# Denominators of two token tiles summed by ScalarE, eight staging places, and the copy of the denominators on VectorE, in a one-core attention and quantized-FFN layer

## The chip, the cores and the metric

The kernel runs on one core of a Trainium2 chip. A core has a matrix engine (TensorE, PE in the profile; its weight loads are listed as PEld), VectorE (DVE), ScalarE (ACT), GpSimd (POOL) and SyncE (SP, which here issues nearly all transfers). Each engine works through its own instructions in order and waits on semaphores of the others. The work memory SBUF and the matrix engine's result memory PSUM both have 128 partitions; PSUM has eight banks of 512 float32 columns.

The metric is the time of the whole kernel on the device in microseconds, the median of several executions. Lower is better.

## What is computed

The input x has 4 batches of 512 tokens with 1024 features. One attention block and one quantized linear layer, each behind a layer norm and with a residual:

```python
q = (ln(x) @ Wq).reshape(b, s, 32, 32)         # 32 heads of 32
k, v = split(ln(x) @ Wkv)                      # one key and one value head for all
scores = einsum('bqhd,bkd->bhqk', q, k) * 32 ** -0.5
scores = where(causal, scores + slope[h] * (pos_k - pos_q), -inf)
attn = softmax(scores, axis=-1)
x = x + einsum('bhqk,bkd->bqhd', attn, v).reshape(b, s, h) @ Wo
w = (unpacked_6bit_codes - zero_point) * scale # 1024 x 1024
x = x + (ln(x) @ w.T + bias)
```

All tensors are float32. The kernel gets that accuracy by splitting operands into a high and a low part and adding two or three products.

## The kernel before

A batch has 4 token tiles of 128 tokens (NT = 4). The 32 heads form 8 groups of 4 (GH = 4, NG = 8). A batch and a group make one *step*; there are 32 steps, and after them 16 token tiles of the output projection and the linear layer. Work of neighbouring steps, of the next batch's preparation and of the first token tiles overlaps.

One step does this:

- `queries` (line 749) computes the group's queries, and their high and low parts go through DRAM into a stacked tile `qs`, below which lie rows that add the position bias and the causal mask of whole key blocks.
- `maxima` (line 806) computes the scores with queries on the partitions: for each token tile t and head h a tile of 128 queries by (t + 1) x 128 keys, in a PSUM bank `s` (two banks). On each tile one VectorE instruction (line 837) adds the mask to the scores, writes the negated sum to `junk` and puts the negated row maximum into a column of `mx`. `mx` is transposed by PE (line 862), split into a high and a low part by ScalarE (line 868, tile mt0) and VectorE (line 873, tile mt1), and both rows are sent by DMA into `qs`, so that the next product has the maximum already subtracted.
- `attention` (line 891) computes the scores again, with the keys on the partitions: key block j against queries j x 128 to 511, into PSUM banks `st` (two banks, line 913). ScalarE takes the exponential into the tiles p0 to p3 (line 923), GpSimd zeroes the part above the diagonal (line 932), and PE multiplies with the values (line 942, `pav`), four heads side by side on four column tiles.
- The softmax denominators come from two places. For the last token tile (queries 384 to 511) ScalarE takes the exponential of the `junk` that line 837 left in a staging tile, with the maximum as bias and with a running sum as second output (line 852), into a column of `own_den`. For the other 384 queries GpSimd adds p1 and p2 onto p0 (line 955, two additions: 4 x 256 and 4 x 128 columns), PE sums over the partitions with a matrix of ones (line 970, `den`, 4 heads x 384 columns), ScalarE copies the result out of PSUM (line 977), and a DMA writes it to `den_d` in DRAM (line 980).
- `invert` (line 984) runs once per batch: PE transposes `own_den`, ScalarE copies it (line 996), a DMA writes these rows to `den_d` (line 999), all denominators of the batch are read into `rec` (line 1007), inverted by VectorE (line 1013) and written to `rden_d` (line 1017).
- `token_tile` (line 1118) multiplies the attention output by these reciprocals and does the output projection (line 1170), the layer norm and the linear layer (line 1289).

Tiles come from pools with a fixed number of buffers. The pool `stg` ("staging", 5 places of 128 x 512 float32) is shared: weights on their way in, `junk` of the last token tile, the attention output `a`, the denominators `d`, codes, and the linear layer's products. `mt` holds two buffers each of mt0 and mt1; `rec` and `zs` (the zero points) have places of their own.

The order of the instructions is not written by hand. Every operation is entered with a due time (in units where a step takes 15), an estimated cost and the tiles it reads and writes. `order` (line 368) lays all operations out by a model of the engines, with 16 different small shifts of the due times, and takes the best by its model. It fixes the order on every engine and on the DMA queue, and which earlier user of a buffer a new one waits for. So an edit of a cost or of a pool size changes the order of the whole program.

The instruction that makes the staged scores and the row maximum, shared by both kernels, in its essence:

```python
nc.vector.tensor_tensor_reduce(
    out=junk()[:, :W], in0=ps()[:, o : o + W], in1=mask()[:, S - W :],
    scale=-1.0, scalar=3e38, op0=ALU.add, op1=ALU.min,
    accum_out=mx()[:, h * NT + t : h * NT + t + 1],
)
```

Of the kernel before, what the change touches and what calls it, by code (L numbers as in the profile page):

```python
# [34 lines left out]
F32 = mybir.dt.float32  # L35
# [4 lines left out]
AF = mybir.ActivationFunctionType  # L40
# [4 lines left out]
P = 128  # L45
NH = 32
HD = 32
GH = 4
S = 512
H = 1024  # L50
# [346 lines left out]
def layer_kernel(  # L397
# [29 lines left out]

    for name, bufs in (
        ("const", 1), ("w", 2 * NG), ("xc", KC + 2), ("x", 4), ("qs", 3), ("q1", 1), ("p0", 2),
        ("pj", 1), ("stg", 5), ("kv", 2), ("small", 4), ("mt", 2), ("rec", 1), ("zs", 1),  # L430
    ):
        pool(name, bufs)
    for name, bufs in (("s", 2), ("st", 2), ("m", 4)):
# [2 lines left out]
    def new(pool_name, tag, shape, dt, name):  # L436

        p, bufs = pools[pool_name]
        return work.item(lambda: p.tile(shape, dt, tag=tag, name=name), (pool_name + tag, bufs))
# [13 lines left out]
    def act(at, n, fn, out, ins, sbuf=False):  # L453
        work.op("ACT", at, n / 1.2 + (90.0 if sbuf else 70.0), fn, out, ins)
# [212 lines left out]
    kv = {}  # L667
# [134 lines left out]
    ROWS = (0, 1, 2, "b")  # L802

    own_den = {}

    def maxima(at, i):
        b = i // NG
        k = kst[b % 2]
        mx = new("small", "mx", [P, GH * NT], F32, f"mx_{i}")
        if i % NG == 0:  # L810
            own_den[b] = new("small", "sump", [P, GH, NG], F32, f"dn_{b}")
        for n, bank in enumerate(S_BANKS):
            ps = new("ps_s", "s", [P, S], F32, f"s_{i}_{n}")
            widths = [(t + 1) * P for t, _ in bank]
            places = [sum(widths[:m]) for m in range(len(bank))]

            def products(ps=ps, bank=bank, widths=widths, places=places):
                for (t, h), W, o in zip(bank, widths, places):
                    q, at = part(i, h)
                    nc.tensor.matmul(  # L820
                        ps()[:, o : o + W], q()[0:R_MAX, at, ts(t, P)], k()[0:R_MAX, :W],
                        start=True, stop=True,
                    )
            pe(
                at + 1.2 * n, widths, products, [ps],
                [
                    (part(i, h)[0], (r, h) if i < DIRECT and r != "b" else r)
                    for _, h in bank for r in ROWS
                ] + [k],
                more=5.0,  # L830
            )
            for (t, h), W, o in zip(bank, widths, places):
                kind = ("stg", "stg") if t == NT - 1 else ("q1", "junk")
                junk = new(*kind, [P, S if t == NT - 1 else S - P], F32, f"junk_{i}_{t}_{h}")
                dve(
                    at + 1.2 * n + 0.3, W,
                    lambda ps=ps, junk=junk, t=t, h=h, W=W, o=o: nc.vector.tensor_tensor_reduce(  # L837
                        out=junk()[:, :W],
                        in0=ps()[:, o : o + W],
                        in1=mask()[:, S - W :],  # L840
                        scale=-1.0,
                        scalar=3e38,
                        op0=ALU.add,
                        op1=ALU.min,
                        accum_out=mx()[:, h * NT + t : h * NT + t + 1],
                    ),
                    [(mx, (t, h)), junk] if t == NT - 1 else [(mx, (t, h))], [ps], more=125.0,
                )
                if t == NT - 1:
                    act(  # L850
                        at + 1.2 * n + 2.0, S + 130,
                        lambda junk=junk, h=h, t=t: nc.scalar.activation(  # L852
                            junk(), junk(), AF.Exp, bias=mx()[:, h * NT + t : h * NT + t + 1],
                            scale=-1.0, accum_out=own_den[b]()[:, h, i % NG : i % NG + 1],
                        ),
                        [junk, (own_den[b], (h, i % NG))], [junk, (mx, (t, h))], sbuf=True,
                    )
        at += 1.2 * len(S_BANKS)
        N = GH * NT
        tr = new("ps_m", "m", [P, P], F32, f"trm_{i}")  # L860
        pe(
            at, [P], lambda: nc.tensor.transpose(tr()[0:N, :], mx(), ident()), [tr], [mx]
        )
        for s in range(2):
            m = new("mt", f"mt{s}", [N, P], F32R, f"mt{s}_{i}")
            if s == 0:
                hi = m
                act(at + 0.2, P, lambda: nc.scalar.copy(hi(), tr()[0:N, :]), [hi], [tr])
            else:
                lo = m  # L870
                dve(
                    at + 0.4, P,
                    lambda: nc.vector.tensor_tensor(
                        lo(), tr()[0:N, :], hi().bitcast(F32), ALU.subtract
                    ),
                    [lo], [tr, hi],
                )
            for h, n, q in qs[i]:
                dma(
                    at + 0.5 + 0.2 * s, 2e3 * n,  # L880
                    lambda m=m, s=s, h=h, n=n, q=q: move(
                        q()[R_MAX + s : R_MAX + s + 1, :, :], m()[h * NT : (h + n) * NT, :]
                    ),
                    [(q, f"m{s}")], [m],
                )
# [5 lines left out]
    def attention(at, i):  # L891
# [54 lines left out]
        for js, when in (((0, 1), 10.4), ((2, 3), 14.4)):  # L946
# [1 line left out]
                at + when, [4.0 * (S - j * P) for j in js], lambda js=js: products(js), [pav],  # L948
                [kv[b]] + [pr[j] for j in js], tiled=True,
            )  # L950
        L = S - P
        for j in range(1, NT - 1):
            def add(j=j):
                d = pr[0]()[:, :, j * P : L]
                nc.gpsimd.tensor_tensor(d, d, pr[j]()[:, :, 0 : L - j * P], ALU.add)  # L955
            pool_op(
                at + (0, 11.4, 15.0, 15.4)[j], 140.0 + 2.16 * GH * (L - j * P), add,
                [pr[0]], [pr[0], pr[j]],
            )
# [14 lines left out]
        pe(at + 20.0, [4.0 * L], sums, [d], [pr[0]], tiled=True)  # L974

        kept = new("stg", "stg", [P, L], F32, f"d_{i}")
        act(at + 25.5, L, lambda: nc.scalar.copy(kept(), d()), [kept], [d])
        dma(
            at + 26.0, 8e3,
            lambda: nc.sync.dma_start(out=den_d[b, :, g, 0:L], in_=kept()[0:P:HD, :]),  # L980
# [3 lines left out]
    def invert(at, b):  # L984

        tr = new("ps_m", "m", [P, P], F32, f"trd_{b}")
        N = GH * NG
        pe(
            at - 14.0, [P],
            lambda: nc.tensor.transpose(  # L990
                tr()[0:N, :], own_den[b]().rearrange("p h g -> p (h g)"), ident()
            ),
            [tr], [own_den[b]],
        )
        rows_ = new("mt", "mt0", [N, P], F32, f"rows_{b}")
        act(at - 13.5, P, lambda: nc.scalar.copy(rows_(), tr()[0:N, :]), [rows_], [tr])
        dma(
            at - 13.0, 16e3,
            lambda: nc.sync.dma_start(
                out=den_d[b].rearrange("h g q -> (h g) q")[:, S - P :], in_=rows_()  # L1000
            ),
            [(den_i[b], "own")], [rows_],
        )
        r = new("rec", "rec", [P, P], F32, f"rec_{b}")
        dma(
            at, 65e3,
            lambda: nc.sync.dma_start(
                out=r(), in_=den_d[b].rearrange("h g (c q) -> (h g c) q", q=P)
            ),
            [r], [den_i[b]],  # L1010
        )
        work.op(
            "DVE", at + 2.5, 840.0, lambda: nc.vector.reciprocal(r(), r()), [r], [r],
        )
        dma(
            at + 4.0, 65e3,
            lambda: nc.sync.dma_start(
                out=rden_d[b].rearrange("h g (c q) -> (h g c) q", q=P), in_=r()
            ),
            [rden_i[b]], [r],  # L1020
        )
# [60 lines left out]
    def ffn_rows(early, at, later):  # L1082

        b1 = new("pj", "p1", [P, 2, HALF], F32, "bias")
        b2 = [new("q1", t, [P, HALF], F32, f"scale_{t}") for t in ("qh", "ql")]
        b3 = new("zs", "zs", [P, 2, HALF], F32, "zs")
        scale = w_scale.rearrange("n o -> (n o)")
        for when, o, size, ap, src in (
            (early, b3, 524e3, lambda: b3().rearrange("p a b -> p (a b)"),
             w_zero.rearrange("n o -> (n o)")),  # L1090
            (at, b2[0], 262e3, b2[0], scale[0:HALF]),
            (at, b2[1], 262e3, b2[1], scale[HALF:H]),
            (later, b1, 524e3, lambda: b1().rearrange("p a b -> p (a b)"), ffn_bias),
        ):
            dma(
                when, size,
                lambda ap=ap, src=src: nc.sync.dma_start(
                    out=ap(), in_=src.partition_broadcast(P)
                ),
                [o], [],  # L1100
            )
        rows["bias"] = [(b1, lambda n=n: b1()[:, n, :]) for n in range(2)]
        rows["scale"] = [(b2[n], b2[n]) for n in range(2)]
        rows["zs"] = [((b3, n), lambda n=n: b3()[:, n, :]) for n in range(2)]
        for n in range(2):
            it, ap = rows["zs"][n]
            dve(
# [315 lines left out]
```

## Time and profile before

| What | Value |
|---|---|
| Median of 3 runs | 810.4 us (809.18, 811.1, 810.4) |
| The profiled execution | 812.18 us |
| Its span, first to last instruction | 810.5 us |
| Mean granted clock of TensorE | 0.997 |
| Line 837 (row maxima, DVE), 512 instructions | 247.5 us busy |
| Line 923 (exponentials, ACT), 352 | 184.5 us busy |
| Line 852 (exponentials with sum, ACT), 128 | 92.0 us busy |
| Line 955 (additions of p, POOL), 64 | 118.1 us busy |
| Line 970 (den, PE), 256 | 27.2 us busy |
| Line 977 (copy of den, ACT), 32 | 15.6 us busy |

The profile was taken from one execution, of 812.18 us; its times are not those of the runs of the median. The page gives the busy time of each engine, the span in 40 slices, the transfers, the chain of work that ended last (followed back from the last instruction, at each step to what released it) and the costliest groups of instructions by line, with their number, their busy time, the mean duration of one in nanoseconds, and the idle time of the engine before them. Two views cut the span into stretches: busy time of every engine in each. The durations of neighbouring rows overlap, on PE and on ScalarE above all, so that a row's duration is longer than the time that it takes from its engine; the distance from one start to the next is the latter.

By slices of 20 us, in tenths, the engines' busy shares are:

```profile
PE   5999989999999999999999999999999999999997
DVE  7576758566777466876476667546876657676765
ACT  5667966778888677898687786541232323332320
POOL 5137633534644333643537684665726535455333
```

Steps run to about 550 us, and the token tiles fill the rest.

### The profile page before, as it was taken

What the parts mean: (1) busy time and instruction counts of PE and PEld (TensorE: products, weight loads), DVE (VectorE), ACT (ScalarE), POOL (GpSimd) and SP (SyncE); (2) the same over time, 40 slices, a digit from 0 to 9 for tenths busy, and PEclk for the clock granted to TensorE, in tenths of its full rate; (3) what the DMA queues carried; (4) which work ended last, traced back from release to release, by engine and by line L of the source; (5) the groups of instructions that cost most, each with busy time, mean ns of one, the idle gap of its engine ahead of it and who ended that gap; (6) DMA issues with size and microseconds to landing.
All of it is one profiled execution on the core that took longest, in us unless ns stands there. A gap on an engine that the chain in (4) does not pass through costs nothing.

```text
span 810.5 us, 13698 instructions
## 1 busy us (share of the span) xinstructions
PE 790.3 (98%) x4468; PEld 591.5 (73%) x4468; DVE 538.3 (66%) x1484; ACT 477.0 (59%) x961; POOL 403.9 (50%) x397
## 2 busy tenths in 40 slices
PE   5999989999999999999999999999999999999997
PEld 4675667677666777677776767677888888888886
DVE  7576758566777466876476667546876657676765
ACT  5667966778888677898687786541232323332320
POOL 5137633534644333643537684665726535455333
PEclk9999999999999999999999999999999999999999
DMA  7257655765834764734767885748666755657321
GB/s 225 57 142 208 181 162 137 202 187 149 240 106 122 202 190 144 233 118 131 202 182 181 241 226 144 249 109 216 183 151 167 153 137 124 160 138 179 86 53 65
DMA packets 131815, 131.31 MB, mean 162 GB/s; under 512 B 42980, under 2 KB 94436, under 8 KB 130720
## 3 DMA queue, kind: packets, MB, share of 16 engines
q1 hardware_dynamic: 131392, 128.49, 58.0%
q0 software_dynamic: 352, 1.96, 0.9%
q8 instruction: 35, 0.57, 0.3%
q14 instruction: 36, 0.29, 0.1%
HBM read 84.27 MB, written 39.06 MB: 152 GB/s over the span
## 4 chain that ended last, share of the span: by engine, by line
PE 90%; DMA 3%; DVE 3%; ACT 1%; issue 1%; POOL 1%; SPq 0%; DVEq 0%; POOLq 0%
PE pq L757 21%; PE po L1170 19%; PE pf L1289 13%; PE st L913 10%; PE s L820 10%; PE pav L942 9%; PE den L970 3%; PE pkv L674 2%; PE tr L656 2%; DVE junk L837 1%; DMA rec<-den_d 1%; DMA wq_st<-in_L_attn_Wq_dram 1%; DMA raw<-rden_d 1%; DMA rden_d<-rec 1%; ACT qs L733 1%
## 5 line engine op out<-in xcount | busy, mean ns | idle before, releaser
L837 DVE CUSTOM_DVE_ANT_0 junk<-s,mask 128x512 f32<-128x512 f32 (+3 forms) x512 | 247.5, 489 | 126.0 <-PE s L820 100.1
L923 ACT ACTIVATE p<-st 128x512 f32<-128x512 f32 (+1 forms) x352 | 184.5, 559 | 65.0 <-PE st L913 60.7
L757 PE MATMUL pq<-xc,wqh 128*128 128x512 f32 x512 | 198.5, 404 | 0.0
L932 POOL TENSOR_SCALAR_AFFINE_SELECT p<-p 128x512 f32<-128x512 f32 x128 | 83.3, 653 | 201.8 <-ACT p L923 195.8
L1170 PE MATMUL po<-woh,aT 128*128 128x512 f32 x512 | 165.4, 391 | 0.0
L820 PE MATMUL s<-kst,qs 124*128 124x512 f32 (+3 forms) x512 | 130.2, 325 | 5.5 <-DMA wq_st<-in_L_attn_Wq_dram 1.6
L913 PE MATMUL st<-qs,kst 126*128 126x512 f32 (+1 forms) x352 | 128.8, 398 | 0.6 <-DMA qs<-mt 0.5
L955 POOL TENSOR_TENSOR p<-p,p 128x1024 f32<-128x1024 f32 x64 | 118.1, 1845 | 12.5 <-PE pav L942 11.7
L820 PEld LDWEIGHTS s<-kst,qs 124*128 124x128 f32 x512 | 91.6, 189 | 40.1 <-DVE mx L837 9.9
L1289 PE MATMUL pf<-wf,xT 128*128 128x512 f32 x512 | 120.5, 391 | 0.1
L757 PEld LDWEIGHTS pq<-xc,wqh 128*128 128x128 f32 x512 | 97.3, 190 | 21.5 <-issue 2.2
L1170 PEld LDWEIGHTS po<-woh,aT 128*128 128x128 f32 x512 | 96.2, 188 | 20.0 <-issue 0.6
L1289 PEld LDWEIGHTS pf<-wf,xT 128*128 128x128 f32 x512 | 95.8, 188 | 20.4 <-DVE xT L473 0.6
L757 PE MATMUL pq<-xc,wql 128*128 128x512 f32 x256 | 101.3, 396 | 0.0
L852 ACT ACTIVATE junk<-junk,mx 128x512 f32<-128x512 f32 x128 | 92.0, 721 | 13.9 <-DVE mx L837 11.3
L1170 PE MATMUL po<-wol,aT 128*128 128x512 f32 x256 | 99.8, 390 | 0.0
L913 PEld LDWEIGHTS st<-qs,kst 126*128 126x128 f32 x352 | 64.1, 189 | 25.9 <-ACT p L923 6.6
L942 PE MATMUL pav<-p,kv 128*32 128x512 f32 (+3 forms) x1024 | 80.8, 437 | 0.3 <-POOL p L932 0.3
L1309 POOL TENSOR_TENSOR x<-x,y 128x512 f32<-128x512 f32 x30 | 42.7, 1426 | 60.8 <-DVE y L1300 58.9
L942 PEld LDWEIGHTS pav<-p,kv 128*32 128x32 f32 x1024 | 28.1, 109 | 44.0 <-issue 30.8
L1170 PEld LDWEIGHTS po<-wol,aT 128*128 128x128 f32 x256 | 48.2, 188 | 9.4
L757 PEld LDWEIGHTS pq<-xc,wql 128*128 128x128 f32 x256 | 49.2, 192 | 6.4
(92 smaller groups left out, 903.2 us busy)
## 6 DMA issues: line engine op xcount, KB each, us to landing
qs<-q_d SPq DMA_DIRECT2D x90, 256.0 KB
x<-_attn_hidden_states_dram SPq DMA_DIRECT2D x31, 512.0 KB
at_d<-a SPq DMA_DIRECT2D x32, 256.0 KB
raw<-at_d SPq DMA_DIRECT2D x16, 512.0 KB
raw<-rden_d SPq DMA_DIRECT2D x64, 128.0 KB
out_dram<-x SPq DMA_DIRECT2D x32, 256.0 KB
q_d<-qh SPq DMA_DIRECT2D x30, 256.0 KB
q_d<-ql SPq DMA_DIRECT2D x30, 256.0 KB
```

The source lines that it names most:

```text
L757: nc.tensor.matmul(pq(), w()[:, c, :], xc[b, c]()[:, s, :], start=(c == 0 and n == 0), stop=(c == KC - 1 and n == 2),)
L820: nc.tensor.matmul(ps()[:, o : o + W], q()[0:R_MAX, at, ts(t, P)], k()[0:R_MAX, :W], start=True, stop=True,)
L837: lambda ps=ps, junk=junk, t=t, h=h, W=W, o=o: nc.vector.tensor_tensor_reduce(out=junk()[:, :W], in0=ps()[:, o : o + W], in1=mask()[:, S - ...
L852: lambda junk=junk, h=h, t=t: nc.scalar.activation(junk(), junk(), AF.Exp, bias=mx()[:, h * NT + t : h * NT + t + 1], scale=-1.0, accum_ou ...
L913: nc.tensor.matmul(ps()[:, place, :], k()[0:R_ALL, ts(j, P)], q()[0:R_ALL, mine, j * P :], start=True, stop=True,)
L923: lambda ps=ps, own=own, j=j: nc.scalar.activation(pr[j]()[:, own, :], ps(), AF.Exp),
L932: nc.gpsimd.affine_select(out=d, in_=d, pattern=[[0, GH], [1, P]], compare_op=ALU.is_ge, fill=0.0, base=0, channel_multiplier=-1,)
L942: nc.tensor.matmul(pav()[ts(h, HD), j * P :], kv[b]()[:, j, :], pr[j]()[:, h, :], start=(j == 0), stop=(j == NT - 1), tile_position=(0, h ...
L955: nc.gpsimd.tensor_tensor(d, d, pr[j]()[:, :, 0 : L - j * P], ALU.add)
L1170: nc.tensor.matmul(po(), aT[s][1]()[:, c, :], w()[:, ts(n, HALF)], start=(c == 0 and m == 0), stop=(c == KC - 1 and m == 2),)
L1289: nc.tensor.matmul(pf(), xT()[:, s, c, :], wf[c]()[:, ts(n, HALF)], start=(c == 0 and s == 0), stop=(c == KC - 1 and s == 1),)
L1309: (nc.vector if last else nc.gpsimd).tensor_tensor(d, d, y(), ALU.add)
```

## The change

The token tiles whose denominators ScalarE sums become two (OWN = 2: queries 256 to 511), so the other way covers 256 queries. The copy of `den` out of PSUM moves from ScalarE to VectorE. The cost entered for the exponential with a sum is raised. `stg` grows from 5 to 8 places; the tiles of `mt` go from two buffers to one; `rec` moves into the buffer of mt1, the zero points into two staging places (loaded and used by halves), and the sums of ScalarE get a place in the pool `kv`, since they are twice as many.

```diff
-        ("pj", 1), ("stg", 5), ("kv", 2), ("small", 4), ("mt", 2), ("rec", 1), ("zs", 1),
+        ("pj", 1), ("stg", 8), ("kv", 2), ("small", 4), ("mt", 1),
...
+    OWN = 2
...
-            own_den[b] = new("small", "sump", [P, GH, NG], F32, f"dn_{b}")
+            own_den[b] = new("kv", "dn", [P, OWN, GH, NG], F32, f"dn_{b}")
...
-                kind = ("stg", "stg") if t == NT - 1 else ("q1", "junk")
-                junk = new(*kind, [P, S if t == NT - 1 else S - P], F32, f"junk_{i}_{t}_{h}")
+                mine = t >= NT - OWN
+                kind = ("stg", "stg") if mine else ("q1", "junk")
+                junk = new(*kind, [P, S if mine else S - OWN * P], F32, f"junk_{i}_{t}_{h}")
...
-                if t == NT - 1:
+                if mine:
                     act(
-                        at + 1.2 * n + 2.0, S + 130,
-                        lambda junk=junk, h=h, t=t: nc.scalar.activation(
-                            junk(), junk(), AF.Exp, bias=mx()[:, h * NT + t : h * NT + t + 1],
-                            scale=-1.0, accum_out=own_den[b]()[:, h, i % NG : i % NG + 1],
+                        at + 1.2 * n + 2.0, W + 220,
+                        lambda junk=junk, h=h, t=t, W=W: nc.scalar.activation(
+                            junk()[:, :W], junk()[:, :W], AF.Exp,
+                            bias=mx()[:, h * NT + t : h * NT + t + 1], scale=-1.0,
+                            accum_out=own_den[b]()[:, t - (NT - OWN), h, i % NG : i % NG + 1],
                         ),
...
-        L = S - P
-        for j in range(1, NT - 1):
+        L = S - OWN * P
+        for j in range(1, NT - OWN):
...
-        act(at + 25.5, L, lambda: nc.scalar.copy(kept(), d()), [kept], [d])
+        dve(at + 25.5, L, lambda: nc.vector.tensor_copy(kept(), d()), [kept], [d])
...
-        N = GH * NG
+        N = OWN * GH * NG
...
-        dma(
-            at - 13.0, 16e3,
-            lambda: nc.sync.dma_start(
-                out=den_d[b].rearrange("h g q -> (h g) q")[:, S - P :], in_=rows_()
-            ),
-            [(den_i[b], "own")], [rows_],
-        )
-        r = new("rec", "rec", [P, P], F32, f"rec_{b}")
+        for t in range(OWN):
+            dma(
+                at - 13.0, 16e3,
+                lambda t=t: nc.sync.dma_start(
+                    out=den_d[b].rearrange("h g q -> (h g) q")[:, ts(NT - OWN + t, P)],
+                    in_=rows_()[ts(t, GH * NG), :],
+                ),
+                [(den_i[b], ("own", t))], [rows_],
+            )
+        r = new("mt", "mt1", [P, P], F32, f"rec_{b}")
...
-        b3 = new("zs", "zs", [P, 2, HALF], F32, "zs")
+        b3 = [new("stg", "stg", [P, HALF], F32, f"zs_{n}") for n in range(2)]
         scale = w_scale.rearrange("n o -> (n o)")
+        zero = w_zero.rearrange("n o -> (n o)")
...
-            (early, b3, 524e3, lambda: b3().rearrange("p a b -> p (a b)"),
-             w_zero.rearrange("n o -> (n o)")),
+            (early, b3[0], 262e3, b3[0], zero[0:HALF]),
+            (early, b3[1], 262e3, b3[1], zero[HALF:H]),
```

## The prediction

> **What bounds the kernel now.** I read the page first, then the windows by stage, the chain of waits by pieces, the groups by shape, the waits, and last the timeline of ScalarE and of the DMA queue. The page's first rows:
>
> ```profile
> span 810.5 us, 13698 instructions
> PE 790.3 (98%) x4468; PEld 591.5 (73%) x4468; DVE 538.3 (66%) x1484; ACT 477.0 (59%) x961; POOL 403.9 (50%) x397
> PE 90%; DMA 3%; DVE 3%; ACT 1%; issue 1%; POOL 1%; SPq 0%; DVEq 0%; POOLq 0%
> ```
>
> The matrix engine is busy 98% of the span and the chain runs through it for 90%. ScalarE's 59% is a mean over two very different stages. The windows part them (engines in the order PE, PEld, DVE, ACT, POOL; then clock, DMA share, GB/s):
>
> ```profile
> 30.00:540.00 510.00, 504.19 (x3188) 356.23 (x3188) 338.43 (x1206) 389.96 (x844) 252.54 (x266) 1.00 0.61 173
> 540.00:810.00 270.00, 265.93 (x1197) 218.66 (x1195) 182.28 (x248) 71.63 (x93) 137.45 (x105) 1.00 0.56 140
> 345.00:360.00 15.00, 15.00 (x92) 11.09 (x91) 10.26 (x40) 14.36 (x31) 7.75 (x11) 1.00 0.29 93
> ```
>
> The attention stage, where the whole change lies, takes 510 us; PE is idle in it for 5.8 us, ScalarE is busy 390.0 us (76%), and in its worst fifteen microseconds 14.4. So PE sets the pace, with ScalarE the next in line. An edit that takes work from PE in this stage pays until ScalarE, or a wait, takes PE's place.
>
> Against this reading stands the Trainium skill, "Perfetto Trace Analysis", section "Identifying the Most-Contended Engine": matmul busy time is a bad measure because matmuls are pipelined, and the share of the weight loads should be taken, while for ScalarE occupancy is fair. By that rule PE stands at 73%, ScalarE would become the most loaded engine of the stage, and the sum below would lose its gain and end at the time before or above it. I go by the pieces of the chain instead, since these are distances from start to start.
>
> **The change, part by part.**
>
> *PE, denominators.* The product at line 970 sums 384 columns for each of four heads; after the change 256. Pieces of the chain (start, duration, what):
>
> ```profile
> 72.72 1.64 PE pav L942 x16
> 81.03 0.78 PE den L970 x8
> 127.59 0.79 PE pav L942 x16
> ```
>
> The first piece of pav is key blocks 0 and 1 (512 and 384 columns, 896 together), the last is blocks 2 and 3 (256 and 128, 384 together). 512 columns more cost 0.85 us, 1.66 ns a column; den's 0.78 for 384 columns fits the same line. 128 columns less save 0.21 us a step, over 32 steps **6.8 us**. The rows give bounds:
>
> ```profile
> L942 PE MATMUL pav<-p,kv 128*32 128x384 f32 x256 | 26.5, 486 | 0.0
> L942 PE MATMUL pav<-p,kv 128*32 128x256 f32 x256 | 20.3, 389 | 0.0
> L970 PE MATMUL den<-p,ones 128*32 128x384 f32 x256 | 27.2, 497 | 0.0
> ```
>
> 97 ns less per instruction, eight per step on four column tiles side by side, is 2 x 97 x 32 = 6.2 us; a third of den's 2.8% of the chain (22.7 us) is 7.6 us. PE is the full engine here, so nothing hides this work and the cut counts in full: -6.8.
>
> *POOL, the sums of p.* Line 955 runs twice a step:
>
> ```profile
> L955 POOL TENSOR_TENSOR p<-p,p 128x1024 f32<-128x1024 f32 x32 | 76.7, 2396 | 11.8 <-PE pav L942 11.7
> L955 POOL TENSOR_TENSOR p<-p,p 128x512 f32<-128x512 f32 x32 | 41.4, 1295 | 0.7
> ```
>
> After it one addition is left, of 4 x 128 columns, the shape of the second row: POOL loses 76.7 us, from 252.5 to about 176 of 510. POOL was not the bound. PE's loads waited for line 955 0.9 us before pav and 0.6 us before den; I take half of this 1.5 as gain, **-0.8** (0 to -1.5).
>
> *ScalarE, the new sums.* 128 exponentials of 384 columns are added (line 852), and 32 copies of den go (line 977). No row shows an exponential of 384 columns from SBUF with a sum. The nearest:
>
> ```profile
> 352.41 0.71 ACT L852 ACTIVATE junk<-junk,mx 128x512 f32<-128x512 f32 x1
> 353.02 0.19 ACT L852 ACTIVATION_READ_ACCUMULATOR junk<-junk,mx 128x1 f32 x1
> 353.12 0.48 ACT L923 ACTIVATE p<-st 128x384 f32<-128x384 f32 x1
> 353.49 0.58 ACT L470 CAST xc<-tr 128x512 fp32r<-128x512 f32 x1
> ```
>
> Rows on ScalarE overlap, so I take distances between starts: 0.71 us for 512 columns with its sum, 0.37 for 384 columns without. These are the ends. Between them lies 0.71 less the width's part, which line 923 shows as 597 - 491 = 106 ns from 512 to 384 columns: 0.60, which I take. 128 x 0.60 = 76.8 us (47 to 91). A den copy held ScalarE 0.36 us (a start at 226.44, the next at 226.80), 32 of them 11.5. Net **+65.3 us** (36 to 79): ScalarE goes from 390.0 to 455 of 510 us, 89% (84 to 92%).
>
> What hides it is ScalarE's idle time of 120 us in the stage, the largest part of it (49.8 of 98.6 us between 60 and 510) waits for line 913. It fits as a mean, but not everywhere. At 1.92 us more per fifteen microseconds, seven windows of the fifteen-microsecond cut go over: those with 13.58, 13.93, 13.16, 13.11, 14.36, 13.63 and 13.24 then exceed 15 by 3.5 us together. Next late would be the exponentials of line 923, then the two score banks that line 913 writes, then PE. Neighbouring windows have room (120 to 135 holds 8.70), and eight staging places let an exponential of line 852 wait for most of a step. I take half, **+1.8** on PE (0 to 3.5 as long as only these windows count).
>
> *The wait the exponential adds.* Line 837 writes a staging place for eight tiles a step instead of four; it waits until ScalarE has released one. Behind it on VectorE stand the other maxima, behind these line 820's two banks, and so PE. Three places more for four tiles more: costed at nothing, since the exponential's place is part of the overrun just priced.
>
> *VectorE, the copy of den.* No plain copy from PSUM of 256 columns is in the trace. Below it lies the 128-column row of line 873 (275 ns), above it line 837's 256 columns (424 ns). Between 275 at 128 and 682 (line 1180) at 512, 256 gives 411: 32 x 0.41 = 13.2 us (8.8 to 13.6), on 338 of 510 us. It is hidden by VectorE's idle time, mainly its 94.7 us of waits for line 820 between 60 and 500. The copy takes over ScalarE's waits for den (1.5 us between 60 and 510), with the maxima queued behind it. The DMA of line 980 is issued as before, 4 KB for 6.
>
> *Inversion and single buffers.* Each batch issues one more small DMA (two halves of the rows), the zero points load in two parts: five more on SP's queue, at 0.42 to 0.43 us (line 999) about 2.1 us of issuing, none on PE's path. The real price is that mt0 and mt1 have one buffer and that the reciprocals now live in mt1. Today their chain has a buffer of its own:
>
> ```profile
> 431.82 0.43 SPq L1007 DMA_DIRECT2D rec<-den_d  x1
> 435.57 0.95 DVE L1013 RECIPROCAL rec<-rec 128x128 f32<-128x128 f32 x1
> 439.15 0.34 SPq L1017 DMA_DIRECT2D rden_d<-rec  x1
> ```
>
> From load to the store's issue 7.3 us; with a landing as long as the load's (3.75) 11.1 us. A step's own use of mt1 is 0.3 to write it, about 0.6 to the issue and up to 3.6 (the chain's wait for qs<-mt at 76.35) to land, 4.5 us. Together 15.6 in a step of 15.2 (line 862 from 45.0 to 517.0 in 31 steps), 0.4 over, in three batches that have steps behind them: **+1.2**, between 0, when load and store follow quickly, and 16.7, when the next step waits for half the chain each time (3 x 5.55). Behind that wait of line 873 stand VectorE's maxima, and line 913 waits for the row.
>
> *Sum.* -6.8 - 0.8 + 1.8 + 1.2 = -4.6. The profiled run took 812.2 us (1.7 around its span), 1.8 above the median 810.4, so 807.6 in a run like the profiled one, and **805.8** against the median.
>
> **The rivals.**
> 1. *ScalarE takes PE's place* (slower). At 89% every late score tile delays what is queued behind it. For it: the 14.36 of 15, only two banks at line 913. Against: today only 4.9 us of PE's loads wait for line 923, at 76%. If a fifth of the 65.3 us falls on PE, 13.1, in place of the 1.8: 810.4 - 7.6 + 13.1 + 1.2 = 817.1. It decides from a tenth exposed on: 7.6 - 1.2 = 6.4 us, where nothing of the gain is left.
> 2. *The reciprocals block mt1* (slower). Upper end 16.7: 810.4 - 7.6 + 1.8 + 16.7 = 821.3. For it: 15.6 in 15.2 us. Against: these transfers today are issued late because nothing presses (rows written at 182.14 leave at 212.41); pressed, they can be placed after a step's own use.
> 3. *Nothing moves.* The 7.6 us are freed and given back in small waits of ScalarE and VectorE, some 0.24 us a step: 810.4. For it: line 837's and 852's chains get longer. Against: PE's idle time of 5.8 us says that it rarely waits.
> 4. *More than the sum.* The order of all instructions is made anew and POOL's relief removes waits: at most PE's 5.8 us of idle time on top, 800.0.
>
> **How the numbers follow.** Chances: my forecast with rival 4, faster, 0.58 (of which 0.12 for rival 4); rival 3, 0.10; rival 1, 0.20; rival 2 and other waits of the new order, 0.12. A measurement tells about 0.2%, 1.6 us, from no change, so faster means under 808.8 and slower over 812.0: 0.58, 0.10, 0.32. The likeliest's own range is 801 to 808.8. The range that should hold 8 in 10 goes from 800 (rival 4) to 818, just past rival 1; outside lie rival 2's end and a larger share of rival 1.
>
> **What would show it.** Right: den pieces of about 0.57 us with 256 columns, 32 rows of line 955, line 852 with 256 rows, ScalarE near 455 us in the stage, PE without new gaps. Rival 1: waits of line 913's loads for ScalarE well over today's. Rival 2: three waits of several microseconds at lines 868 to 885. The prediction is wrong if the stage, measured from the first line-862 row to the last, does not shorten by some 4 us, or if PE's idle time in it grows past 10 us.

## The result, and the profile after

| | before | after |
|---|---|---|
| Median of 20 runs each | 809.75 us (808.51 to 813.64) | 812.97 us (809.47 to 817.23) |
| Ratio after to before | | 1.003, 95% interval 1.0017 to 1.0043 |
| The profiled execution | 812.18 us, clock 0.997 | 811.64 us, clock 0.992 |

The changed kernel is 0.3% slower; 805.8 was forecast, faster. The time lies in the range and on the wrong side. The two profiled executions don't show the difference of the medians: that of before lies 2.4 us above its median, that of after 1.3 us below. They show what the difference is made of, and the experiments put a price on it. The line numbers of the changed kernel are one to six higher: 820 is now 821, 837 is 839, 852 is 854, 862 is 865, 913 is 916, 923 is 926, 955 is 958, 970 is 973, 977 is 980, 1170 is 1176 and 1180 is 1186.

The page of after, its first rows and the shares of its chain:

```profile
span 809.9 us, 13957 instructions
PE 783.4 (97%) x4468; PEld 594.5 (73%) x4468; DVE 542.6 (67%) x1516; ACT 531.0 (66%) x1185; POOL 329.3 (41%) x365
PE 85%; ACT 3%; DMA 3%; DVE 2%; POOL 1%; issue 1%; SPq 1%; DVEq 0%; POOLq 0%
```

The work went where the change sends it. PE is busy 6.9 us less (790.3 before), POOL 74.6 less, ScalarE 54.0 more. The span is only 0.6 us shorter, and PE's share of the chain fell from 90 to 85%: PE has gaps that it did not have. The groups by shape, for the lines of the change:

```profile
L854 ACT ACTIVATE junk<-junk,mx 128x384 f32<-128x384 f32 x128 | 78.7, 616 | 0.5 <-DVE mx L839 0.3
L958 POOL TENSOR_TENSOR p<-p,p 128x512 f32<-128x512 f32 x32 | 41.7, 1303 | 24.5 <-PE pav L945 24.5
L973 PE MATMUL den<-p,ones 128*32 128x256 f32 x256 | 20.3, 389 | 0.3 <-POOL p L958 0.3
L980 DVE COPY d<-den 128x256 f32<-128x256 f32 x32 | 13.4, 418 | 13.2 <-PE den L973 6.3 <-DMA at_d<-a 6.0 <-POOL wol L544 0.9
```

The four operations have nearly the sizes that were forecast: den's matmuls 389 ns for 497, the second row of line 955 as the only one left, 418 ns for a copy (411 forecast), and 616 ns for the new exponential. What is new to the eye is at the end of the last row: one of the 32 copies waited 6.0 us for `at_d<-a`, a transfer that had to release its staging place.

The waits of PE (who waited, for whom: us, times, longest):

```profile
PE tr L656 <- DVE x L627: 8.1, 1, 8.1
PE po L1176 <- DVE x L1186: 4.2, 1, 4.2
PE s L821 <- DMA q_d<-ql: 2.3, 1, 2.3
```

The first is the start of the program and stands in before too. The other two are new, one wait each. The two longest of before are:

```profile
PE tr L656 <- DVE x L627: 8.2, 1, 8.2
PE s L820 <- DMA wq_st<-in_L_attn_Wq_dram: 1.6, 1, 1.6
```

The windows of after show where the new waits are, and that they cost more than their own length (columns as in the prediction; the clock is the third number from the end):

```profile
30.00:540.00 510.00, 502.08 (x3212) 362.94 (x3212) 345.55 (x1242) 444.14 (x1068) 180.05 (x235) 0.99 0.63 173
...
45.00:75.00 30.00, 26.97 (x139) 18.76 (x138) 18.86 (x75) 24.45 (x64) 11.88 (x13) 0.89 0.62 165
...
540.00:570.00 30.00, 25.78 (x129) 20.35 (x128) 21.57 (x22) 3.40 (x5) 21.30 (x13) 0.94 0.86 214
```

Between 45 and 75 us the granted clock averages 0.89 of full speed, between 540 and 570 it averages 0.94. The clock record has two stretches at half speed there: 6.8 us long from 56.7 on, which begins within the wait that ends at 58.07, and 3.4 us long from 558.5 on, which begins as the other wait ends. In them the products of 512 columns start 427 ns apart, outside them about 230. So half speed costs half of the time that PE works in it, 5.5 and 3.4 us: 2.7 and 1.7 us. Before has one such stretch, 3.4 us from 109.1 on, behind a gap of 1.6 us.

The whole account of PE, from the trace: the distance from each matmul's start to the next one's, summed by what the matmul computes, in us. "Both moved" is the experiment h2 below, the changed kernel with both waits removed.

```
                 before    after   after - before   both moved
den               24.2      16.5        -7.7           16.5
pav               78.3      75.7        -2.6           75.0
pq, high weight  128.0     129.5        +1.5          129.2
st                87.9      89.9        +2.0           89.0
s                 87.5      88.6        +1.1           88.5
po, high weight  117.1     122.7        +5.6          118.9
all others       274.5     273.9        -0.6          273.5
sum              797.5     796.9        -0.7          790.6
```

den brings 7.7 us, the cut that the change is made of. It is given back: +5.6 at the output projection, where one distance alone is 4.4 too long and the half clock adds the rest, and +4.6 over pq, st and s, which hold the wait in the ramp and the matmuls behind it at half clock.

**The wait in the ramp**, the first steps. ScalarE's timeline, of after and then of before (start, duration):

```profile
40.49 0.62 ACT L854 ACTIVATE junk<-junk,mx 128x384 f32<-128x384 f32 x1
...
41.10 0.60 ACT L854 ACTIVATE junk<-junk,mx 128x384 f32<-128x384 f32 x1
...
42.43 0.62 ACT L854 ACTIVATE junk<-junk,mx 128x384 f32<-128x384 f32 x1
...
43.04 0.60 ACT L854 ACTIVATE junk<-junk,mx 128x384 f32<-128x384 f32 x1
...
44.97 0.59 ACT L470 CAST qh<-pq 128x512 fp32r<-128x512 f32 x1
```

```profile
43.37 0.59 ACT L470 CAST qh<-pq 128x512 fp32r<-128x512 f32 x1 [0.34 <-PE pq L757]
```

The cast `qh` of the third step's queries stands behind four of the new exponentials and starts 1.6 us later. Its low part `ql` follows on VectorE behind the maxima, both go through DRAM, and PE's next scores wait 2.3 us. The row of the waits names `q_d<-ql`, but a product of scores reads `qs`: by the semaphores of the trace it waits for the load `qs<-q_d` of the low part, which is issued at 51.25, when the store of `ql` has landed, and lands at 57.82.

**The wait at the passage** from the steps to the token tiles, on VectorE and on POOL:

```profile
546.43 0.43 DVE L980 COPY d<-den 128x256 f32<-128x256 f32 x1 [5.98 <-DMA at_d<-a]
...
552.05 1.77 DVE L1277 SCALAR_TENSOR_TENSOR x<-zs,sumx,x 128x512 f32<-128x512 f32 x1
554.99 2.81 DVE L1277 SCALAR_TENSOR_TENSOR x<-zs,sumx,x 128x512 f32<-128x512 f32 x1 [1.17 <-POOL x L1273]
557.72 1.27 DVE L1186 TENSOR_TENSOR x<-x,po 128x512 f32<-128x512 f32 x2
```

```profile
546.35 5.23 POOL L1273 TENSOR_TENSOR x<-x,bias 128x512 f32<-128x512 f32 x3
551.54 1.73 POOL L1315 TENSOR_TENSOR x<-x,y 128x512 f32<-128x512 f32 x1
553.35 1.60 POOL L1273 TENSOR_TENSOR x<-x,bias 128x512 f32<-128x512 f32 x1
```

Line 1186 adds the output projection onto x and so releases its PSUM bank; PE has finished that product by 554.3 and needs the bank. The two additions of line 1186 stand in VectorE's order behind two of line 1277 (zero point times a row sum, onto x). The second of these waits 1.17 us for POOL's fourth bias addition (line 1273) and then takes 2.81 us. PE goes on at 558.54, 4.2 us late.

### The profile page after: what moved, and what is told of

Same layout as the page of the kernel before. It is cut to its first block, busy times and chain, and to the rows that moved or that the text cites. A ratio compares the mean times of both kernels' runs of the same rounds, so it can differ in the third digit from the quotient of the medians.

```text
span 809.9 us, 13957 instructions
## 1 busy us (share of the span) xinstructions
PE 783.4 (97%) x4468; PEld 594.5 (73%) x4468; DVE 542.6 (67%) x1516; ACT 531.0 (66%) x1185; POOL 329.3 (41%) x365
## 4 chain that ended last, share of the span: by engine, by line
PE 85%; ACT 3%; DMA 3%; DVE 2%; POOL 1%; issue 1%; SPq 1%; DVEq 0%; POOLq 0%
PE po L1176 20%; PE pq L757 19%; PE pf L1295 13%; PE st L916 9%; PE s L821 9%; PE pav L945 8%; PE den L973 2%; DMA qs<-qr_d 2%; PE pkv L674 1%; ACT junk L854 1%; ACT p L926 1%; PE tr L656 1%; POOL x L1273 1%; DMA raw<-rden_d 1%; DVE junk L839 1%
## 5 line engine op out<-in xcount | busy, mean ns | idle before, releaser
L839 DVE CUSTOM_DVE_ANT_0 junk<-s,mask 128x384 f32<-128x384 f32 (+3 forms) x512 | 236.7, 488 | 117.1 <-PE s L821 105.5
L854 ACT ACTIVATE junk<-junk,mx 128x384 f32<-128x384 f32 (+1 forms) x256 | 170.0, 668 | 6.1 <-DVE mx L839 5.8
L821 PE MATMUL s<-kst,qs 124*128 124x128 f32 (+3 forms) x512 | 130.0, 325 | 5.3 <-DMA q_d<-ql 2.3
L1295 PE MATMUL pf<-wf,xT 128*128 128x512 f32 x512 | 122.2, 391 | 0.0
L1315 POOL TENSOR_TENSOR x<-x,y 128x512 f32<-128x512 f32 x30 | 44.4, 1480 | 55.5 <-DVE y L1306 55.5
L470 ACT CAST aT<-raw 128x1024 fp32r<-128x1024 f32 x16 | 16.8, 1049 | 67.9 <-POOL raw L1153 62.7
```

The costliest lines, as they stand in the source:

```text
L470: act(at, n, lambda: nc.scalar.copy(hi(), src()), [hi_it], [src_it], sbuf=port)
L821: nc.tensor.matmul(ps()[:, o : o + W], q()[0:R_MAX, at, ts(t, P)], k()[0:R_MAX, :W], start=True, stop=True,)
L854: lambda junk=junk, h=h, t=t, W=W: nc.scalar.activation(junk()[:, :W], junk()[:, :W], AF.Exp, bias=mx()[:, h * NT + t : h * NT + t + 1], s ...
L1295: nc.tensor.matmul(pf(), xT()[:, s, c, :], wf[c]()[:, ts(n, HALF)], start=(c == 0 and s == 0), stop=(c == KC - 1 and s == 1),)
L1315: (nc.vector if last else nc.gpsimd).tensor_tensor(d, d, y(), ALU.add)
```

## The experiments

Theories at the start: that the loss belongs to the edits (ScalarE's load, or the copy of den on VectorE, whose wait of 5.98 us stands ahead of the passage), or to the new order of all instructions, drawn once for each kernel. Where an expectation uses letters, A blames the copy's wait for the passage (in experiment 4 the late queries for the wait in the ramp), B the draw of the order, C ScalarE's load, D a cause other than the one that the run moves, E the load of line 1136 at the head of SP's queue, and F the two additions of line 1277.

Two kinds of edit are used. One gives the planner other random numbers, so that the same operations with the same costs get another order. The other keeps the order and moves a few operations in it, by number:

```python
    ordered = work.order()

    def put(numbers, after):
        moved = [work.ops[n] for n in numbers]
        rest = [o for o in ordered if o not in moved]
        at = rest.index(work.ops[after]) + 1
        ordered[:] = rest[:at] + moved + rest[at:]
```

**1. The copy of den by itself.** In the changed kernel it goes back to ScalarE (e1); in the kernel before it goes to VectorE (e5). Both are planned anew.

```diff
-        dve(at + 25.5, L, lambda: nc.vector.tensor_copy(kept(), d()), [kept], [d])
+        act(at + 25.5, L, lambda: nc.scalar.copy(kept(), d()), [kept], [d])
```

> The changed kernel with the copy of den back on ScalarE; all else as changed. Theory A (the gain on PE is real, and is given back in a stall of 4.4 us at the passage to the token tiles, which begins with VectorE's copy of den waiting 6.0 us for a staging place, and in one during the first steps, each followed by a stretch at half clock): the wait of the copy is now ScalarE's, VectorE's later rows come in time, the stall at the passage is under 1 us, and the time is 806 to 809. Theory B (the new order of all instructions is a draw, good or bad): any time from 804 to 816, with stalls at other places. Theory C (ScalarE is too full): 11.5 us more on ScalarE make it slower than the changed kernel, 815 or more, and PE's waits for lines 926 and 854 grow.

> The kernel before with one part of the change alone: den is copied out of PSUM by VectorE (384 columns). Theory A: VectorE waits for a staging place in this copy (5 places, so more often than with 8), waits of 1 to 6 us at the copy, and 2 to 5 us slower than before. Theory B: a new draw, 806 to 815. Theory C: ScalarE is relieved by 11.5 us and the time is the same or lower, 807 to 810.

e1 took 807.03 us, 0.9964 of before (0.9949 to 0.9979); e5 took 817.34, 1.0088 (1.0065 to 1.0111). Read alone, they say that the copy on VectorE costs 6 to 8 us. The time of e5 lies above all that had been expected. But in e1 both waits are gone, the one in the ramp too, which has nothing to do with den (a new one of 2.2 us stands elsewhere); and in e5 PE does not wait for the copy, but for other things (1.8 us for `qs<-mt`, 1.8 for `qs<-qr_d`). Each edit made a new order, and with it new waits. Without the next group of runs these two can't be told from chance; what the copy is worth alone stays open.

**2. The same kernels in other orders.** Four more orders of each kernel: 100, 200, 300 or 400 is added to the numbers that start the random shifts.

```diff
-            rnd = random.Random(n)
+            rnd = random.Random(100 + n)
```

> The changed kernel; only the seeds of the 16 random shifts of due times differ, so the order is another draw. Theory A with the stalls as consequences of the edit: the same two stalls come back, 811 to 815. Theory B: PE's total for den and pav is again some 10 us less than in the kernel before, but the stalls lie elsewhere or are gone; the time differs from the changed kernel's by 2 us or more in either direction. Theory C: within 1.5 us of the changed kernel, since ScalarE's load is the same.

> The kernel before; only the seeds of the random shifts differ. Theory B: the order it had was a good draw, and this one differs by 2 us or more, more likely slower (812 to 816). Theories A and C: within 1.5 us of the kernel before, 808 to 812.

> The changed kernel with a third set of seeds. Theory B (the edit saves some 8 to 10 us of PE's work in every order, and the order's draw moves either kernel by several us): PE's total for den is 16 to 18 us as in the other two draws, for pav 75 to 77, and the time lies between 799 and 812, with 805 the middle. Theory C (ScalarE's load costs as much as it saves): 810 or more.

> The kernel before with a third set of seeds. Theory B: PE's total for den is 24 to 25.5 us, the time lies between 809 and 819, with 814 the middle, so that the given order is among the best draws. Theory C: within 2 us of 810.

> The changed kernel with a fourth set of seeds. Theory B: den 16 to 18 us in PE's total, the time between 799 and 813, and with the other three draws a mean near 805 to 807. Theory C: 810 or more.

> The kernel before with a fourth set of seeds. Theory B: den 24 to 25.5 us in PE's total, the time between 809 and 819, and a mean of the four draws near 814 to 815. Theory C: a mean of the four near 810.

> The changed kernel with a fifth set of seeds. Theory B: 799 to 813, den 16 to 18 us. Theory C (no gain apart from the draw): as likely over 811 as under.

> The kernel before with a fifth set of seeds. Theory B: 809 to 819, den 24 to 25.5 us. Theory C: as likely under 811 as over.

| order | kernel before: median us, ratio to before (95%) | changed kernel: median us, ratio to before (95%) |
|---|---|---|
| given | 809.75 | 812.97, 1.003 (1.0017 to 1.0043) |
| 100 | 815.96, 1.0071 (1.0044 to 1.0098) | 802.20, 0.9907 (0.9882 to 0.9932) |
| 200 | 816.18, 1.0070 (1.0052 to 1.0089) | 808.09, 0.9966 (0.9946 to 0.9987) |
| 300 | 811.66, 1.0009 (0.9993 to 1.0025) | 801.79, 0.9888 (0.9862 to 0.9915) |
| 400 | 816.49, 1.0077 (1.0059 to 1.0094) | 809.69, 0.9983 (0.9966 to 1.0000) |
| mean | 814.0 | 806.9 |

The ratios are to runs of before made beside each experiment, with medians of 810.0 to 810.4 us. The ranges of theory B held but for two small misses: den took 18.2 us of PE in order 400 of the changed kernel (16 to 18 expected), and the first four orders of before have a mean of 813.4 (814 to 815).

The given order of before is the best of its five, the given order of after the worst of its five. The means differ by 7.1 us; with the spread of the orders (4.1 us, both kernels pooled) the 95% interval of that is 1.1 to 13.0 us (8 degrees of freedom). So in an average order the change makes the kernel faster, by about what den's columns bring: over the five orders of each, PE's start-to-start sum for den averages 24.92 us before and 17.07 after, 7.86 of the 8.86 us by which the sums of all matmuls differ. The orders with 100 and 300 beat both kernels, and their intervals overlap; either is the version to use. Of the order with 300, the first rows of the page and PE's longest waits:

```profile
span 800.3 us, 13938 instructions
PE 780.5 (98%) x4468; PEld 590.6 (74%) x4468; DVE 551.1 (69%) x1516; ACT 532.4 (67%) x1185; POOL 331.0 (41%) x365
```

```profile
PE tr L656 <- DVE x L627: 7.8, 1, 7.8
PE s L821 <- ACT qs L745: 1.4, 2, 0.7
PE st L916 <- DMA qs<-mt: 1.1, 3, 0.6
```

ScalarE carries the same load as in after (532.4 and 531.0 us). Behind the start of the program no single wait is over 0.7 us. That ScalarE's load must cost what the change brings is thereby excluded.

**3. The copy of den, order kept.** The last step's copy goes later in VectorE's order (17 instructions by the trace), behind line 1186, with nothing else moved: `put([3392], 3656)`.

> The changed kernel with its order of instructions held, except that the last step's copy of den on VectorE stands 21 VectorE instructions later, behind the residual additions of line 1186 that PE waits for. Theory A (the stall of 4.4 us at the passage comes from this copy's 6.0 us wait for a staging place): PE's wait for line 1186 goes, the stretch at half clock after it too, 4 to 6 us less: 807 to 809. Theory D (the stall at the passage has another cause, such as GpSimd's chain or the late reciprocals): PE's gap of some 4 us stays near 554 and the time within 1.5 us of the changed kernel's.

812.86 us, 1.0025 (1.0006 to 1.0043): no change from after, and PE's wait is still there.

```profile
PE po L1176 <- DVE x L1186: 4.4, 1, 4.4
```

```profile
546.89 1.23 DVE L473 TENSOR_TENSOR aT<-raw,aT 128x1024 fp32r<-128x1024 f32 x1 [7.21 <-ACT aT L470]
```

VectorE no longer waits for the copy's staging place. The instruction that stood behind the copy now waits for ScalarE, 7.21 us, and starts at 546.89, where it had started at 547.51. So the copy's wait of 6 us had covered another wait that ended almost as late, and did not set when line 1186 ran; theory A is out.

**4. The queries of the third step first, order kept.** Its casts and stores go ahead of the four exponentials: `put([417, 418, 419, 420, 260, 264, 268, 256], 416)`.

> The changed kernel with its order held, except that in the third step the queries' high and low part and their two stores stand ahead of the first step's exponentials with sums (four of two token tiles) and maxima. Theory A (the stall of 2.4 us near 55 and the 6.8 us at half clock behind it come from queries that leave late behind the new exponentials): the wait for the queries goes or is under 0.5 us, so does the stretch at half clock, 3 to 6 us less: 807 to 810. Theory D (the round trip through DRAM is late for its own reasons): the gap moves by less than 1 us, and the time is within 1.5 us of the changed kernel's.

809.67 us, 0.9991 (0.9975 to 1.0008), 3.3 below after. The window of the ramp:

```profile
45.00:75.00 30.00, 28.86 (x167) 20.03 (x167) 21.18 (x82) 29.18 (x78) 14.32 (x16) 1.00 0.68 176
```

PE starts 167 matmuls for 139 in the same thirty microseconds, at the full clock. The wait for `q_d<-ql` is gone. Wait and half clock were 5.0 us together (2.3 + 2.7); 3.3 come out. Part of the difference is the wait of line 865 for VectorE's maxima, 1.6 us in place of 0.8, and one of 0.4 us for `qs<-q_d`; part may be that the half clock differs from run to run (after: mean clock 0.991 to 0.995 in its 20 runs, 814.0 to 817.2 us in the four at 0.991, 809.5 to 813.2 in the four at 0.995).

**5. SP's queue, order kept.** At the passage SP waited 15.6 us at line 1136's load, with three transfers behind it that VectorE and ScalarE wait for. These go ahead of it: `put([3212, 3457, 3458], 3565)`. f6 does this and experiment 4 together.

> The changed kernel with its order held, except that on SP's queue three transfers at the passage (one store of the attention output and the two loads of the zero points) stand ahead of the token tile's load of line 1136, which waits 15.6 us for VectorE with them behind it. Theory E (the stall of 4.4 us at the passage comes from this wait at the head of SP's queue: held up for 15.6 us, the transfers then go all at once and land late): ScalarE's wait of 2.7 us for the zero points goes, PE's wait for line 1186 falls to 2 us or less, the time is 808 to 811. Theory D (the lateness lies in the token tile's own load and products, whatever stands behind them): PE's wait stays at 4 us or more and the time within 1.5 us of the changed kernel's 813.

> The two moves of order together: the third step's queries first, and the three transfers ahead of the token tile's load. Theory E: both stalls small, 803 to 808. Theory D: the second move does nothing, and the time is that of the first move alone, 809 to 811.

f4: 810.93 us, 1.0012 (0.9988 to 1.0036). f6: 808.32, 0.9975 (0.9959 to 0.9991). PE's wait for line 1186 shrinks to 3.6 us in f4, where at most 2 had been expected, and is 3.9 in f6. The time of f4 is in E's range and 2.0 us below after, that of f6 1.4 below experiment 4; the intervals overlap in both cases. Theory E explains a little of the wait, not its body.

**6. The residual first, order kept.** The two additions of line 1277 and the stores behind them go behind the two of line 1186: `put([3605, 3607, 3608, 3609], 3636)`. h2 does this and experiment 4 together.

> The changed kernel with its order held, except that two additions of the zero points (line 1277) and their two stores stand behind the two residual additions of line 1186 that PE waits for. Theory F (the stall at the passage is VectorE's order: line 1186 stands behind line 1277, which waits for GpSimd's bias additions): PE's wait for line 1186 falls under 1 us, the stretch at half clock near 555 goes in the profile, 3 to 6 us less than the changed kernel's 813: 807 to 810. Theory D (line 1186 is late for its own reason): PE's wait stays over 3 us and the time is within 1.5 us of 813.

> The changed kernel with two moves of order: the third step's queries ahead of the exponentials, and the residual additions ahead of line 1277. Theory F: both stalls go, 803 to 807, which is 6 to 10 us less than the changed kernel. Theory D: 809 to 811, as with the first move alone.

h1: 807.92 us, 0.9975 (0.9960 to 0.9990), 5.0 below after. h2: 805.50, 0.9946 (0.9930 to 0.9961), 7.5 below after. The mean clock of all runs is 0.9931 in after, 0.9972 in h1 and 0.9990 in h2; what is missing to 1, times the span, is 5.6, 2.3 and 0.8 us, so that up to 4.8 of the 7.5 us are half clock that no longer comes. It may be less, since this share also counts half speed while PE stands still: of 6.2 us in the profiled execution of after, 4.4 fall on working PE. The rest are the waits, less what is left of them or takes their place in h2, 2.8 us: the longest wait of line 865 is 1.6 us in place of 0.8, `qs<-q_d` is new, and 1.4 us stay at line 1186.

```profile
PE trm L865 <- DVE mx L839: 1.9, 2, 1.6
PE po L1176 <- DVE x L1186: 1.4, 1, 1.4
PE s L821 <- DMA qs<-q_d: 0.6, 1, 0.6
```

VectorE's timeline in h1, PE's wait, and the window of the passage:

```profile
553.49 1.28 DVE L1186 TENSOR_TENSOR x<-x,po 128x512 f32<-128x512 f32 x2 [2.22 <-DMA x<-_attn_hidden_states_dram]
554.69 2.64 DVE L1277 SCALAR_TENSOR_TENSOR x<-zs,sumx,x 128x512 f32<-128x512 f32 x2
```

```profile
PE po L1176 <- DVE x L1186: 0.8, 1, 0.8
```

```profile
540.00:570.00 30.00, 29.03 (x149) 22.84 (x148) 20.93 (x27) 4.82 (x6) 20.57 (x13) 1.00 0.83 215
```

Line 1186 runs 4.2 us earlier, PE's wait falls from 4.2 to 0.8 us, and the clock stays at 1.00; 149 matmuls start in the window for 129. That is theory F, and the gain of 5.0 us is near what the profiles show, 3.4 of wait and 1.7 of half clock. The same operations, the same costs and nearly the same order then run in 805.5 us.

## Why the prediction was wrong, point by point

- **PE, denominators**: forecast -6.8 (6.2 to 7.6), measured -7.7 from start to start. Right, a little small.
- **POOL**: forecast 76.7 us of work less and 0.8 on PE. POOL lost 74.6. pav lost 2.6 us, but in before it holds a wait of 1.6 us for a load of weights and one of 0.3 us, which leaves 0.7; in the mean of five orders pav lost 0.3.
- **ScalarE**: forecast +65.3 (36 to 79), measured +54.0, in the stage 444.1 of 510 us or 87% (89 forecast). The 0.60 us from start to start were right (42.43 to 43.04, 43.04 to 43.64). The rest is most likely work next to it that overlaps; no run parts it. The price of the overrun, +1.8, can't be seen by itself: the products into the two score banks (st) cost 2.0 more, and 0.6 more in the mean of five orders. The reading that was set against the sum, by the share of the weight loads, did not hold: by it ScalarE, at 76% of the stage, stood above PE's loads, 70%, already in before (73% is their share of the whole span), and would now be the bound, at 87%; yet the orders with 100 and 300 carry the same load and gain. The section cited there names a second measure beside that share, the use of the array's peak, which was not worked out.
- **VectorE**: forecast 13.2 us of copies and no time on PE; measured 13.4, and experiment 3 shows that even the copy that waited 6 us did not hold PE up.
- **Single buffers**: forecast +1.2 (0 to 16.7). No wait of some microseconds shows at the lines that make mt (871 to 888); the reciprocals fit between the steps.
- **Rival 1**: needed 13.1 us of ScalarE on PE. Between 60 and 510 us PE's loads wait for line 926 for 6.6 us in place of 4.9, and PE itself for 0.6; and the orders at 802 us carry the same load. Out. **Rival 2** is out with the single buffers. **Rival 3** gives nearly the measured time, for another reason: the gain is not given back in small waits at every step but at two places. **Rival 4**, a new order that removes waits (800.0 at best), is what the orders 100 and 300 show (802.2 and 801.8), without the given order having it.

**The step that failed** is the frame of the sum: it was made in the order of before, each edit set against the idle time of the same stage, while "the order of all instructions is made anew" was counted as a gain only (rival 4, at most 5.8 us) and as a loss only inside the 0.12 for "rival 2 and other waits of the new order", without a price. The criterion "if the stage [...] does not shorten by some 4 us" was then met against the forecast: 471.9 us before (45.2 to 517.1), 472.3 after (44.2 to 516.5). The runs put in its place: the edits are worth about -7 in a mean order, as the sum's -4.6 had it in sign and nearly in size; a new order adds a draw with a spread of 4 us to each kernel; the given order of before lies 4.3 below the mean of its five, the given order of after 6.0 above. 4.3 + 6.0 - 7.1 = +3.2 is the difference of the medians. (This splits the difference; the runs that show its cause in the given order are h1 and h2.) That the one given order is the best of five and the other the worst is luck as far as the runs show, with a chance of 1 in 25. In the given order of after the excess is two waits, of 2.3 and 4.2 us, and the half clock that comes with them, 2.7 and 1.7 in the profiled execution: 10.9 together. When both are moved, 7.5 come back; 2.8 us of waits stay or take their place. That h2's 805.5 is so near the forecast 805.8 is in part luck too: den brought more than was forecast, and these 2.8 us were in no sum.

The profile of before could have warned. Its stage holds 5.8 us of idle PE, a few single waits; that is what one good order has, and one profile doesn't tell how good it is among orders. The end below of the range was read off it (800.0), an end above for the same cause was not worked out.

What stays open: what the copy on VectorE is worth by itself, and whether the eight staging places pay; and five orders each are few, so that the 7.1 is known only to within 5.9. Two token tiles without the other parts of the change were not tried.

## What to carry to other kernels

Where a planner makes the order anew, compare several orders of both versions, or hold the order and move the operations in question, before an edit of under a per cent is credited or blamed: here the order alone spread both kernels over 7 and 11 us. Follow a wait of the bounding engine back along the releasing engine's own order, and test the suspect by moving it: the most conspicuous wait (6 us at line 980) was innocent, the culprit stood right ahead of the late instruction. A gap on PE is to be priced with the clock behind it.

## What the runs showed of the hardware

The granted clock drops to 0.5 in pieces of 3.41 or 6.83 us when PE has stood still. Between 30 us and the end, over all 18 traces, each of the five gaps of 3.5 us and more has such a piece beginning in it or within 0.2 us of its end (3.55, 3.87, 4.22, 4.37 and 4.48 us); four of the six between 1.9 and 2.7 us have one within them or at most 1.5 us behind them, and one of the seven between 1.5 and 1.7. Two pieces (g1 at 221.1 us, i1 at 555.4) come behind several shorter gaps, none over 1.1 us. The same gap can go either way: 2.28 us at 55.8 in after had 6.83 us of half clock, from 56.7 on, 2.14 us at 56.1 in h1, with the same instructions up to there, had none. So a wait of 2.3 us cost 2.7 us more than itself in one execution, and nothing more in another.

The clock record shows what a gap's length alone does not. In all 18 traces every stretch between two changes of the clock, at full speed or at half, is a whole multiple of 3.413 us (in after 40.96, 6.83, 494.93, 3.41 and 245.76), so the changes fall on instants 3.413 us apart, and these lie elsewhere in the program in each execution. Cut at these instants from 30 us to PE's last matmul, the traces have 4044 pieces at full speed. Ten leave PE idle for 1.74 us or more in all, and each of them has half speed in the piece behind it. Of the others, with at most 1.62 us, only two have: 1.48 us in after, where the wait in the ramp begins, and 1.15 us in g1.

The Trainium skill, "TensorE: Matmul & The Clock Gate", Part 1, states half rate after an idle window of about 3.4 us, with the window running free of the program; the spacing of 3.413 us here agrees, and so does it that the same gap can go either way. The table in the section "Why this matters for your kernels" allows gaps of up to about 3 us between bursts; five shorter ones here were followed by the half clock, and the measurement decides.
